# Expert weights carried in the scattered rows, and gathers that accumulate into x

## The chip, the cores and the metric

The kernel runs on one core of a Trainium2 chip. The metric is the device time of one execution in microseconds, the median of several runs. Engines are named as in the profile: PE is TensorE (PEld its weight loads), DVE is VectorE, ACT is ScalarE, POOL is GpSimd, SP is SyncE, which only issues transfers here.

## The reference

Two transformer blocks on 8 sequences of 512 tokens, 256 features each. Each block is pre-normalized attention (16 heads of 16) and a pre-normalized mixture of experts, both added to x.

```
x = x + L0_attention(layernorm(x))           # causal, rope, 4 key/value heads
x = x + L0_experts(layernorm(x))             # 32 experts of 96, top 8 of softmax
x = x + L1_attention(layernorm(x))           # causal, 16 heads, biases
x = x + L1_experts(layernorm(x))             # 16 experts of 176, top 2, and a shared expert of 352

# experts, both layers; layer 0 divides the 8 weights by their sum
rw, sel = top_k(softmax(x @ router.T), K)
for e in experts:
    w_e = sum(where(sel == e, rw, 0))
    acc = acc + (silu(x @ wg[e]) * (x @ wu[e])) @ wd[e] * w_e
```

## The kernel before

The kernel computes only the chosen experts. Each layer goes in two stages, so that the program has four of them, with the results at the end:

- **Attention 0** (0 to about 656 us of the profile). `pipeline` runs over the 8 sequences. While the heads of sequence b are computed (24 steps: scores on PE, exponentials on ACT, masks on DVE L658), `before(b + 1)` prepares the next sequence and `finish(b - 1)` ends the last: output projection, then `after0`, which normalizes (`layernorm`), turns the rows and calls `route`.
- **route** (L313) computes the router's logits, chooses the experts and gives every pair of token and expert a row in a buffer in device memory (`lay.xg`), where each expert has a slab of its own. POOL scatters the normalized rows there: for each block of 128 tokens and each of the k experts one indirect transfer of 128 rows of 256 numbers (L384), 32 for a sequence of layer 0 and 8 of layer 1. After that, DVE finds the weight of each of the k rows by comparing the rows' numbers with those of all experts (`same`, L394 to L399) and keeps them in `lay.weights`.
- **Experts 0** (`experts`, about 656 to 1172 us). A job is two tiles of 128 rows. Five stages follow one another with lags of 0, 4, 5, 6 and 7 steps: `load` (SP reads the tiles from `lay.xg`; every 8 tiles, expert numbers become register values that address the weights), `turn_x` (PE transposes, DVE copies), `gate_up` (PE; ACT takes silu, DVE multiplies with the other half, L1141 in layer 0 and L1138 in layer 1), `turn_h` (PE, DVE), `down` (PE, ACT copies, SP writes the rows to `lay.yg`). The order on PE is the order of the program here (a manual schedule); on the other engines a planner orders instructions by their dependencies and priorities. Sequences are in two parts (4 and 4 in layer 0, 5 and 3 in layer 1), so that the results of the first part can be collected while the second is computed. `Beside` spreads this work over the steps.
- **Collecting**. `gathers` (L1183) has POOL fetch the k result rows of each token with an indirect transfer of 128 rows (L1199) into a small ring of tiles, and `add` (L1205) has DVE multiply by the weights and add to x (L1210). `gathered` keeps `AHEAD` = 4 pairs of gathers waiting for their adds. `add` may be ordered behind a given DVE instruction (`behind`): the last copy of the experts, or the last mask of the attention. For layer 0, the first four sequences are collected during the experts (`x_in_ring`), the others during attention 1 (`ahead1`), two sequences ahead of where they are used. In layer 1, `results` also turns x and writes the output.
- **Attention 1** (about 1172 to 1770 us), as attention 0, with the shared expert in `after1`. At its start POOL fills the tiles of v with ones (`v_tiles`, L791), for which it needs memory that the experts release.
- **Experts 1 and the results** (from 1770 us to the end at 2055.8).

[...] The tiles of x are a ring of four; sequences that are not in it stand in device memory (`x_after`).

Of the kernel before, what the change touches and what calls it, by code (L numbers as in the profile page):

```python
# [7 lines left out]
F32 = mybir.dt.float32  # L8
# [64 lines left out]
AHEAD = 4  # L73
# [18 lines left out]
def two_blocks_kernel(  # L92
# [56 lines left out]
    zeros = cpool.tile([P, D], F32, tag="zeros", name="zeros")  # L149
# [60 lines left out]
    class Layer:  # L210
        def __init__(self, n, part, seqs, n_e, k, gu):
# [10 lines left out]
            self.xg = drp.tile([n_e * self.cap + P, D], F32, tag=f"xg{name}", name=f"xg{name}")  # L222
# [16 lines left out]
            self.weights = routes("weights", k, F32)  # L239
# [41 lines left out]
    def layernorm(x, lnp, name, tag="xn", bufs=1):  # L281

        stats = lnp.tile([P, NT, 6], F32, tag="stats", name=f"stats_{name}")
        mv = lnp.tile([P, NT, 2], F32, tag="mv", name=f"mv_{name}")
        for t in range(NT):
            nc.vector.bn_stats(out=stats[:, t, :], in_=x[:, t, :])
            nc.vector.bn_aggr(out=mv[:, t, :], in_=stats[:, t, :])
        rstd = inverse_root(mv[:, :, 1], lnp, name)
        xn = lnp.tile([P, NT, D], F32, tag=tag, name=f"xn_{name}", bufs=bufs)
        for t in range(NT):  # L290
            nc.vector.tensor_scalar(
                xn[:, t, :], x[:, t, :], mv[:, t, 0:1], rstd[:, t : t + 1], ALU.subtract, ALU.mult
            )
        return xn
# [17 lines left out]
    def ffn_parts(smp, bank):  # L312
        def route(n, b, xn, xT, name, again):  # L313
# [36 lines left out]
            wt = smp.tile([P, NT, n_e], F32, tag="wt", name=f"wt_{name}")  # L350
# [31 lines left out]
            for t in range(NT):  # L382
# [7 lines left out]
            yield  # L390

            same = smp.tile([P, NT, k, n_e], F32, tag="same", name=f"same_{name}", bufs=1)
            shape = [P, NT, k, n_e]
            nc.vector.tensor_tensor(  # L394
                same, key.unsqueeze(2).to_broadcast(shape), keys[:, :, :k].unsqueeze(3).to_broadcast(shape), ALU.is_equal
            )
            nc.vector.tensor_tensor(same, same, wt.unsqueeze(2).to_broadcast(shape), ALU.mult)
            weights = lay.weights[b]
            nc.vector.tensor_reduce(weights, same, AX.X, ALU.add)  # L399
# [224 lines left out]
    class Attention:  # L624
# [6 lines left out]
        def __init__(self, n, late, ptp, ps, bank, wo):  # L631
            self.n, self.fine, self.late, self.ptp, self.ps, self.bank, self.wo = n, fines[n], late, ptp, ps, bank, wo
            self.heads, self.otok, self.rec = {}, {}, {}
            self.last = iter(())
            self.masked = None
# [107 lines left out]
    def pipeline(att, before, after, n_before, n_after, till, ahead=None):  # L743
# [12 lines left out]
        for b in range(NB):  # L756
# [4 lines left out]
            for n, _ in enumerate(att.steps(b)):  # L761
                while made_post < n_after * (n + 1 - STEPS) // (till - STEPS):
                    next(post, None)
                    made_post += 1
                while made_pre < n_before * (n + 1) // (n_steps - 2):
                    next(pre, None)
                    made_pre += 1
                next(early, None)
# [162 lines left out]
    def fast1(w, v1s, lnp, atp, late, ptp, ps, bank):  # L931
        wv, wo, vb, ob, qkb = (w[n] for n in ("v", "o", "vb", "ob", "qkb"))
        att = Attention(1, late, ptp, ps, bank, wo)

        def before(b):
            x, name = xs[b], f"a1_{b}"
            xn = layernorm(x, lnp, name)
# [42 lines left out]
    def tables(lay, small, bank, again, beside=None):  # L980
# [3 lines left out]
        lay.offi = tpool.tile([1, 2, most], I32, tag=f"offi{lay.part}", name=f"offi{name}")[:, :, :n_t]  # L984
# [41 lines left out]
        offf = small.tile([1, 2, n_t], F32, tag="offf", name=f"offf_{name}", bufs=1)  # L1026
        dn = D if lay.n == 0 else ND1 * D
        nc.vector.tensor_scalar(offf[:, 0, :], ex, float(n_e - 1), float(lay.gu), ALU.min, ALU.mult)
        nc.vector.tensor_scalar(offf[:, 1, :], ex, float(n_e - 1), float(dn), ALU.min, ALU.mult)
# [3 lines left out]
        for lo in range(0, n_e, 8):  # L1033
            with tc.issue_after(beside.load) if beside else ExitStack():
# [5 lines left out]
                for rows in at:  # L1040
                    inst = nc.sync.dma_start(out=lay.xg[rows, :], in_=zeros)
                    tc.declare_no_dep(inst.ins, group=group, reason="these rows are no token's")
                    tc.add_to_no_dep_group(group, inst.ins)
            yield

    class Beside:


        def __init__(self, *items):
            self.items = []  # L1050
            for item in items:
                self.add(*item)
            self.last = None
            self.load = None
# [16 lines left out]
    def experts(n, gu, dn, mp, ps, again, beside):  # L1071
# [10 lines left out]
        def registers(lay, i):  # L1082
# [7 lines left out]
                    lay.offi[0:1, j, i : min(i + RB, lay.tiles(again))], engines=[ENG.PE], min_val=0, max_val=(lay.n_e - 1) * step,  # L1090
                    skip_runtime_bounds_check_because="an expert's number is at most the last one's",
                )[1]
                for j, step in enumerate((lay.gu, w_dn))
# [6 lines left out]
        def load(lay, i):  # L1100
# [3 lines left out]
            xg = mp.tile([P, 2, D], F32, tag="xg", name=f"xg_{name}_{part}_{i}", bufs=6)  # L1104
# [4 lines left out]
        def turn_x(lay, i):  # L1109
            part = lay.part  # L1110
            xg = made.pop(("xg", part, i))
# [8 lines left out]
        def gate_up(lay, i):  # L1120
            part = lay.part
            xT = made.pop(("xT", part, i))
# [4 lines left out]
            else:  # L1127
                gus = [ps.tile([P, 2 * inner], F32, tag="gu", name=f"gu_{name}_{part}_{i + j}") for j in range(2)]
            for j in range(2):
# [6 lines left out]
                if n:  # L1136
                    nc.scalar.activation(h[:, j, :], gus[j][:, :inner], AF.Silu)
                    nc.vector.tensor_tensor(h[:, j, :], h[:, j, :], gus[j][:, inner:], ALU.mult)  # L1138
            if n == 0:
                nc.scalar.activation(h, whole[:, :, :inner], AF.Silu)  # L1140
                nc.vector.tensor_tensor(h, h, whole[:, :, inner:], ALU.mult)  # L1141
# [39 lines left out]
    PART = 2  # L1181

    def gathers(n, b, gat, again=""):  # L1183
# [11 lines left out]
        for t in range(NT):  # L1195
            for lo in range(0, k, PART):
                g = gat.tile([P, PART, D], F32, tag="gath", name=f"g{name}_{t}_{lo}")
                for i in range(PART):
                    nc.gpsimd.indirect_dma_start(  # L1199
                        out=g[:, i, :], out_offset=None, in_=lay.yg[: lay.tiles(bool(again)) * P, :],  # L1200
                        in_offset=bass.IndirectOffsetOnAxis(ap=rows[:, t, lo + i : lo + i + 1], axis=0),
                    )
                yield b, t, lo, g, lay.weights[b]

    def add(part, behind):  # L1205

        b, t, lo, g, weights = part
        with tc.issue_after(behind()) if behind() else ExitStack():
            for i in range(PART):
                nc.vector.scalar_tensor_tensor(  # L1210
                    xs[b][:, t, :], g[:, i, :], weights[:, t, lo + i : lo + i + 1], xs[b][:, t, :], ALU.mult, ALU.add
                )

    def gathered(n, b, gat, again="", behind=lambda: None):

        wait = []
        made = gathers(n, b, gat, again)
        while True:
            if len(wait) == AHEAD:
                add(wait.pop(0), behind)  # L1220
            part = next(made, None)
            if part is None:
                break
            wait.append(part)
            yield
        while wait:
            add(wait.pop(0), behind)
            yield
# [50 lines left out]
    def results(seqs, gat, op, ps, again="", behind=lambda: None):  # L1279


        def begin(b):
            fetch_x(b, x_after[1], f"c1{again}")
            yield from gathers(1, b, gat, again)

        made = {}
        for b, after in zip(seqs, [*seqs[1:], None]):
            if b not in made:
                made[b] = []
                for part in begin(b):  # L1290
                    made[b].append(part)
                    yield
            if after is not None:
                made[after] = []
                for part in begin(after):
                    made[after].append(part)
                    yield
            for part in made.pop(b):
                add(part, behind)
                yield  # L1300
# [43 lines left out]
    def all_experts(n, gw, gat, again=False, weights=()):  # L1344
# [6 lines left out]
        with ExitStack() as s:  # L1351
# [11 lines left out]
            def behind():  # L1363
                return beside.last

            def x_in_ring():
                for b in range(SPLIT[0]):
                    fetch_x(b, x_after[0], f"a1{g}")
                    yield from gathered(0, b, gat, g, behind)
# [22 lines left out]
            if n == 0:  # L1392
                beside.add(done, end, SPLIT[0] * 21, x_in_ring())
            else:
                beside.add(done, end, SPLIT[1] * 10, results(range(SPLIT[1]), gat, gat, ps, g, behind))
            experts(n, gw, dw, mp, ps, again, beside)


    PARTS = 4
    with ExitStack() as s:  # L1400
# [6 lines left out]
        def after0(b):  # L1407
            name = f"f0_{b}"
            kept = keep_x(b, x_after[0]) if b < NB - 1 else None
            xn = layernorm(xs[b], lnp, name, "xn_rows", 2)  # L1410
# [14 lines left out]
    with ExitStack() as s1:  # L1425
        wp1 = s1.enter_context(tc.tile_pool(name="attn_w1", bufs=1, reuse_waits="tile"))
        gat = s1.enter_context(tc.tile_pool(name="gather", bufs=AHEAD, reuse_waits="tile"))
        w1, loads1 = weights1(wp1)
        all_experts(0, gw0, gat, weights=loads1)
        with ExitStack() as s:  # L1430
# [3 lines left out]
            att, before = fast1(w1, v1s, lnp, atp, late, ptp, ps, bank)  # L1434
# [3 lines left out]
            def ahead1(b):  # L1438
                if b >= SPLIT[0]:
# [3 lines left out]
                    yield from gathered(0, b, gat, behind=lambda: att.masked)  # L1443

            def after1(b):
                name = f"f1_{b}"
                xn = layernorm(xs[b], lnp, name, "xn_rows")
# [9 lines left out]
            pipeline(att, before, after1, 15, 17, NCK * STEPS, ahead1)  # L1457
# [3 lines left out]
    def last_part(gw, again=""):  # L1461
        with ExitStack() as s:
            gat = s.enter_context(tc.tile_pool(name=f"gather1{again}", bufs=2 * NT, reuse_waits="tile"))
# [8 lines left out]
    def general0():  # L1472
        with ExitStack() as s:
# [8 lines left out]
            def all_of(b, name):  # L1482
# [3 lines left out]
                xn = layernorm(xs[b], lnp, name)  # L1486
# [7 lines left out]
    def general1(gat):  # L1494
        with ExitStack() as s:
# [20 lines left out]
            def all_of(b, name):  # L1516
                if b >= SPLIT[0]:
                    fetch_x(b, x_after[0], "a1g")
                    yield from gathered(0, b, gat, "g")
                yield from attention1(b, w)  # L1520
                xn = layernorm(xs[b], lnp, name)
# [13 lines left out]
    with tc.If(v != 0):  # L1535
        with ExitStack() as s:
            gat = s.enter_context(tc.tile_pool(name="gatherg", bufs=AHEAD, reuse_waits="tile"))
# [166 lines left out]
```

## Time and profile before

| | us |
|---|---|
| median of 3 runs | 1711.17 |
| lowest, highest | 1704.48, 1711.67 |
| the profiled execution | 2057.66 |
| its span | 2055.8 |

The profiled execution is longer than the timed ones. Busy times by stage are these, in us (gathers and scatters are POOL's indirect transfers in that stretch):

| stretch | PE | DVE | ACT | POOL | transfers of POOL | DMA share |
|---|---|---|---|---|---|---|
| attention 0, 0 to 656 | 396.6 | 339.0 | 205.5 | 247.3 | 242 scatters | 0.28 |
| attention 1, 1150 to 1770 | 552.2 | 366.1 | 255.7 | 199.1 | 128 gathers, 64 scatters | 0.26 |
| experts 1, 1770 to 1930 | 154.3 | 68.7 | 35.8 | 13.5 | 15 gathers | 0.42 |
| the end, 1930 to 2056 | 83.7 | 53.2 | 25.7 | 48.6 | 50 gathers | 0.48 |

The columns are busy time; matmuls are pipelined, and the ends of their records are modelled. The DMA share is the mean busy share of the core's 16 DMA engines.

### The profile page before, as it was taken

How to read it: one execution, taken by the hardware profiler on the slowest of the kernel's cores; microseconds unless marked ns; L12 is line 12 of the kernel's file. 1: busy time of each engine (PE TensorE's matmuls, PEld its weight loads, DVE VectorE, ACT ScalarE, POOL GpSimd, SP SyncE). 2: the span in 40 equal slices, each digit the busy share in tenths (PEclk: the TensorE clock that was granted, in tenths of full speed). 3: DMA queues.
4: the chain of work that ended last, by engine and by line, in shares of the span. 5: the costliest groups of instructions: out<-in, count | busy, mean ns of one | idle time of the engine just before them, and what ended most of it. 6: DMA issues, size and time to landing. Idle time of an engine off the chain costs nothing.

```text
span 2055.8 us, 31001 instructions
## 1 busy us (share of the span) xinstructions
PE 1619.5 (79%) x10180; PEld 1070.6 (52%) x10180; DVE 1088.5 (53%) x3311; ACT 649.2 (32%) x867; POOL 645.7 (31%) x662
## 2 busy tenths in 40 slices
PE   5967467477533799997988989788897998999892
PEld 3424234233212699987877735444443545677671
DVE  5657256266342444445766546667566554543352
ACT  3524234234210233322222254343342454122121
POOL 0052452442565000015444301545444111100434
PEclk9978688687775899999999999898998998999995
DMA  1123233321224567667777500332332212443454
GB/s 60 40 93 85 85 95 106 127 73 57 93 97 151 159 224 229 188 186 209 219 213 215 171 8 22 111 113 72 111 101 63 79 42 70 151 144 114 136 172 136
DMA packets 230552, 247.73 MB, mean 121 GB/s; under 512 B 80212, under 2 KB 203220, under 8 KB 230388
## 3 DMA queue, kind: packets, MB, share of 16 engines
q1 hardware_dynamic: 199172, 160.88, 25.8%
q0 software_dynamic: 30720, 83.93, 12.8%
q8 instruction: 89, 1.46, 0.3%
q10 hardware_dynamic: 496, 0.85, 0.1%
q14 instruction: 75, 0.61, 0.1%
HBM read 127.06 MB, written 118.49 MB: 119 GB/s over the span
## 4 chain that ended last, share of the span: by engine, by line
PE 58%; another core or an unknown queue 8%; DVE 8%; issue 6%; ACT 2%; DMA 1%; ACTq 0%; SPq 0%; DVEq 0%
PE gu_m L1132 14%; PE y_m L1162 10%; PE st_a L647 5%; PE xgT_m L1115 4%; PE o_a L670 4%; PE hT_m L1151 3%; PE sg_f L411 2%; PE sy_f L424 2%; PE su_f L411 2%; PE q_a L963 2%; PE y_a L736 2%; PE lg_f L320 1%; PE k_a L968 1%; PE v_a L950 1%
## 5 line engine op out<-in xcount | busy, mean ns | idle before, releaser
L1199 POOL DMA_INDIRECT g<-yg,yrows x320 | 315.5, 986 | 705.0 <-DMA xg_m<-xg 231.2
L384 POOL DMA_INDIRECT xg<-xn_f,rows_f x320 | 325.3, 1017 | 671.5 <-DVE rows_f L381 336.6
L652 ACT ACTIVATE p_a<-st_a 128x2048 f32<-128x2048 f32 (+1 forms) x192 | 305.9, 1593 | 434.6 <-PE st_a L647 228.9
L1132 PE MATMUL gu_m<-gw,xgTs_m 128*128 x1552 | 348.6, 370 | 28.5 <-DVE xgTs_m L1117 14.5
L647 PE MATMUL st_a<-qT_a,kT_a 32*128 32x512 f32 (+3 forms) x2048 | 214.4, 504 | 122.4 <-ACT p_a L652 68.4
L1132 PEld LDWEIGHTS gu_m<-gw,xgTs_m 128*128 128x128 f32 x1552 | 268.4, 199 | 60.9 <-issue 19.9
L1162 PE MATMUL y_m<-dw,hTs_m 96*128 (+1 forms) x952 | 244.8, 388 | 1.5 <-DVE hTs_m L1152 1.5
L670 PE MATMUL o_a<-p_a,v 128*32 128x512 f32 (+3 forms) x2048 | 206.3, 479 | 18.6 <-DVE p_a L658 11.8
L658 DVE TENSOR_TENSOR p_a<-p_a,causal 128x512 f32<-128x512 f32 x256 | 170.3, 682 | 87.5 <-ACT p_a L652 70.3
L647 PEld LDWEIGHTS st_a<-qT_a,kT_a 32*128 32x128 f32 x2048 | 95.1, 200 | 228.4 <-issue 107.9
L1117 DVE COPY xgTs_m<-xgT_m 128x512 f32<-128x512 f32 x194 | 133.5, 688 | 147.7 <-PE xgT_m L1115 102.4
L1167 ACT COPY ys_m<-y_m 128x512 f32<-128x512 f32 x194 | 113.6, 585 | 239.9 <-PE y_m L1162 148.9
L1162 PEld LDWEIGHTS y_m<-dw,hTs_m 96*128 96x128 f32 (+1 forms) x952 | 170.0, 195 | 18.3 <-DVE hTs_m L1152 1.8
L1152 DVE COPY hTs_m<-hT_m 96x256 f32<-96x256 f32 (+1 forms) x194 | 92.7, 478 | 129.2 <-PE hT_m L1151 85.7
L1115 PE MATMUL xgT_m<-ident,xg_m 128*128 128x128 f32 x776 | 122.8, 281 | 17.6 <-DMA xg_m<-xg 12.6
L1140 ACT ACTIVATE h_m<-gu_m 128x192 f32<-128x192 f32 x150 | 49.5, 331 | 254.4 <-PE gu_m L1132 142.7
L1210 DVE SCALAR_TENSOR_TENSOR x_a<-g,weights,x_a 128x256 f32<-128x256 f32 x256 | 122.1, 477 | 4.1 <-issue 0.6
L670 PEld LDWEIGHTS o_a<-p_a,v 128*32 128x32 f32 x2048 | 52.2, 113 | 137.8 <-issue 88.7
L1115 PEld LDWEIGHTS xgT_m<-ident,xg_m 128*128 128x128 f32 x776 | 99.1, 145 | 42.3 <-issue 17.0
L1151 PE MATMUL hT_m<-ident,h_m 128*96 128x128 f32 (+1 forms) x476 | 87.4, 282 | 40.8 <-DVE h_m L1141 19.4
L676 DVE COPY osb_a<-o_a 128x512 f32<-128x512 f32 x64 | 43.9, 687 | 137.1 <-remote 93.2
L736 PE MATMUL y_a<-wo,oT_a 128*128 128x256 f32 x256 | 75.1, 431 | 39.4 <-ACT oT_a L729 37.7
(203 smaller groups left out, 1775.5 us busy)
## 6 DMA issues: line engine op xcount, KB each, us to landing
xg_m<-xg SPq DMA_DIRECT2D x388, 128.0 KB
yg<-ys_m SPq DMA_DIRECT2D x194, 256.0 KB
xg<-zeros SPq DMA_DIRECT2D x100, 128.0 KB
xg<-xn_f,rows_f POOLq DMA_INDIRECT x320
g<-yg,yrows POOLq DMA_INDIRECT x320
xf<-in_x_dram SPq DMA_DIRECT2D x8, 512.0 KB
x_after<-x_in SPq DMA_DIRECT2D x8, 512.0 KB
x_a<-x_after SPq DMA_DIRECT2D x8, 512.0 KB
```

The lines of the kernel that those rows point to most:

```text
L384: inst = nc.gpsimd.indirect_dma_start(out=lay.xg, out_offset=bass.IndirectOffsetOnAxis(ap=rows[:, t, i : i + 1], axis=0), in_=xn[:, t, :], ...
L647: nc.tensor.matmul(st[:, g, at : at + T - j * P], kT[r, j * P : (j + 1) * P], qT[r, j * P :], start=True, stop=True,)
L652: nc.scalar.activation(pt, st[:, :, :width], AF.Exp, scale=SCALE)
L658: self.masked = nc.vector.tensor_tensor(d, d, causal.unsqueeze(1).to_broadcast([P, NG, P]), ALU.mult).ins
L670: nc.tensor.matmul(o[32 * g : 32 * g + 32, j * P :], v1[:, j, v_at + g * (DH + 1) :][:, :32], probs[n][:, g, at : at + T - j * P], start=( ...
L1115: nc.tensor.transpose(tr[:, j, c, :], xg[:, j, c * P : (c + 1) * P], ident)
L1117: nc.vector.tensor_copy(xT, tr)
L1132: nc.tensor.matmul(gus[j], xT[:, j, c, :], gu[:, bass.ds(at + c * 2 * inner, 2 * inner)], start=(c == 0), stop=(c == ND - 1),)
L1151: nc.tensor.transpose(hp[:n_in, q, j, :], h[:, j, lo : lo + n_in], ident)
L1162: nc.tensor.matmul(y[:, j, :], hT[:n_in, q, j, :], dn[:n_in, bass.ds(at + q * D, D)], start=(q == 0), stop=(q == n_ch - 1),)
L1199: nc.gpsimd.indirect_dma_start(out=g[:, i, :], out_offset=None, in_=lay.yg[: lay.tiles(bool(again)) * P, :], in_offset=bass.IndirectOffset ...
L1210: nc.vector.scalar_tensor_tensor(xs[b][:, t, :], g[:, i, :], weights[:, t, lo + i : lo + i + 1], xs[b][:, t, :], ALU.mult, ALU.add)
```

## The change

- The buffer's rows become D + n_e wide (288 numbers in layer 0, 272 in layer 1). `layernorm` leaves n_e columns spare, `route` writes the token's weights of all experts there, and the scatter carries them along. The search for the k weights on DVE is gone, and so is `lay.weights`.
- In `gate_up` the product of silu and the other half is also multiplied by the weight of the row. The column is the tile's expert, a register value, which is now loaded on DVE too. In layer 0 one instruction for two tiles becomes two.
- The tiles that `load` reads are kept until `gate_up`; seven buffers instead of six.
- Layer 0's gathers accumulate straight into x in the DMA (`compute_op=ALU.add`), in the order expert rank, then block of 128 tokens. There is no ring of tiles and no add on DVE. In the experts' stage, all four sequences' x is fetched first.
- In layer 1's results, gathers stay plain, into whole tiles of four blocks for each of the two ranks, and DVE adds two blocks at a time without a weight.
- The first normalization of layer 1's attention is ordered behind masks: its statistics come after the last mask that was traced (for the first sequence, after the last copy of layer 0's experts). `before` starts four steps later in a sequence.

```diff
-            self.xg = drp.tile([n_e * self.cap + P, D], F32, tag=f"xg{name}", name=f"xg{name}")
+            self.width = D + n_e
+            self.xg = drp.tile([n_e * self.cap + P, self.width], F32, tag=f"xg{name}", name=f"xg{name}")
...
         for t in range(NT):
-            nc.vector.bn_stats(out=stats[:, t, :], in_=x[:, t, :])
+            with tc.issue_after(behind) if behind else ExitStack():
+                nc.vector.bn_stats(out=stats[:, t, :], in_=x[:, t, :])
...
-            wt = smp.tile([P, NT, n_e], F32, tag="wt", name=f"wt_{name}")
+            wt = xn[:, :, D : D + n_e]
...
-            same = smp.tile([P, NT, k, n_e], F32, tag="same", name=f"same_{name}", bufs=1)
...
-            nc.vector.tensor_reduce(weights, same, AX.X, ALU.add)
...
-                while made_pre < n_before * (n + 1) // (n_steps - 2):
+                while made_pre < n_before * (n + 1 - lead) // (n_steps - 2 - lead):
...
-            xg = mp.tile([P, 2, D], F32, tag="xg", name=f"xg_{name}_{part}_{i}", bufs=6)
+            xg = mp.tile([P, 2, lay.width], F32, tag="xg", name=f"xg_{name}_{part}_{i}", bufs=7)
...
+            def scaled(j):
+                nc.vector.scalar_tensor_tensor(
+                    h[:, j, :], h[:, j, :], xg[:, j, D:][:, bass.ds(offs[part, i + j][2], 1)], gus[j][:, inner:],
+                    ALU.mult, ALU.mult,
+                )
...
             if n == 0:
                 nc.scalar.activation(h, whole[:, :, :inner], AF.Silu)
-                nc.vector.tensor_tensor(h, h, whole[:, :, inner:], ALU.mult)
+                for j in range(2):
+                    scaled(j)
...
-        for t in range(NT):
-            for lo in range(0, k, PART):
-                g = gat.tile([P, PART, D], F32, tag="gath", name=f"g{name}_{t}_{lo}")
-                for i in range(PART):
-                    nc.gpsimd.indirect_dma_start(
...
+        for i in range(k):
+            for t in range(NT):
+                yield i, t, lay.yg[: lay.tiles(bool(again)) * P, :], bass.IndirectOffsetOnAxis(ap=rows[:, t, i : i + 1], axis=0)
+
+    def gathers(n, b, gat, again=""):
+        for i, t, yg, rows in gather_rows(n, b, gat, again):
+            nc.gpsimd.indirect_dma_start(
+                out=xs[b][:, t, :], out_offset=None, in_=yg, in_offset=rows, compute_op=ALU.add
+            )
+            if t % 2:
+                yield
...
-    def add(part, behind):
-        b, t, lo, g, weights = part
-        with tc.issue_after(behind()) if behind() else ExitStack():
-            for i in range(PART):
-                nc.vector.scalar_tensor_tensor(
-                    xs[b][:, t, :], g[:, i, :], weights[:, t, lo + i : lo + i + 1], xs[b][:, t, :], ALU.mult, ALU.add
-                )
...
+            made[b] = [gat.tile([P, NT, D], F32, tag="gath", name=f"g1{again}_{b}_{i}", bufs=2 * K1) for i in range(K1)]
...
+                    with tc.issue_after(behind()) if behind() else ExitStack():
+                        nc.vector.tensor_tensor(
+                            xs[b][:, lo : lo + 2, :], xs[b][:, lo : lo + 2, :], g[:, lo : lo + 2, :], ALU.add
+                        )
...
                 for b in range(SPLIT[0]):
                     fetch_x(b, x_after[0], f"a1{g}")
-                    yield from gathered(0, b, gat, g, behind)
+                yield
+                for b in range(SPLIT[0]):
+                    yield from gathers(0, b, gat, g)
...
-            pipeline(att, before, after1, 15, 17, NCK * STEPS, ahead1)
+            pipeline(att, before, after1, 15, 17, NCK * STEPS, ahead1, 4)
```

## The prediction

> **What bounds the kernel now.** I read the page first (busy shares, slices), then the chain that ended last, the busy time by stage, the groups of the operations that change, and the timeline where POOL hands over from one stage to the next.
>
> ```profile
> span 2055.8 us, 31001 instructions
> ...
> PE 1619.5 (79%) x10180; PEld 1070.6 (52%) x10180; DVE 1088.5 (53%) x3311; ACT 649.2 (32%) x867; POOL 645.7 (31%) x662
> ...
> PE   5967467477533799997988989788897998999892
> ...
> POOL 0052452442565000015444301545444111100434
> ```
>
> PE has most of the time, and its slices are low just where POOL's are not zero. By stage (us, then busy time of PE, PEld, DVE, ACT, POOL, the granted clock, the DMA share, GB/s):
>
> ```profile
> 690.00:905.00 215.00, 210.90 (x1330) 195.02 (x1329) 106.96 (x260) 66.59 (x147) 0.34 (x1) 0.99 0.66 202
> 905.00:1150.00 245.00, 207.20 (x1164) 184.82 (x1163) 148.28 (x377) 56.99 (x128) 123.53 (x128) 0.92 0.72 212
> ```
>
> ```profile
> 1441.30:1521.80 80.50, 68.61 (x417) 35.50 (x417) 51.34 (x162) 31.04 (x28) 40.76 (x41) 0.89 0.34 97
> ...
> 1602.70:1667.00 64.30, 64.08 (x431) 33.34 (x427) 35.24 (x120) 30.87 (x28) 8.99 (x9) 0.97 0.10 36
> ```
>
> The first pair is layer 0's experts without and with gathers, the second pair one sequence of layer 1's attention with and without. Without gathers PE is 98% and 99.7% busy. A step of the experts is then 2.825 us (distance of L1141 in the timeline); with gathers the mean is 245 us over 64 steps, 3.83. So gathers with their adds cost 64 x 1.0 = 61 us there and 4 x 16 = 65 us in attention.
>
> What does it, POOL's transfers or DVE's adds? The chain has long pieces in the scatter phases of attention 0, where there is no add at all:
>
> ```profile
> 374.30 21.23 another core or an unknown queue
> ...
> 530.21 23.46 another core or an unknown queue
> ```
>
> POOL issues 32 scatters without a pause from 349.6 to 391.3 and from 507.5 to 549.6; PE, ACT and DVE stand still until about 4 us after such a run. Runs of 8 to 12 gathers bring halts of 3 to 7 us. Most of the loss is therefore POOL's runs, the smaller part DVE. The profiled execution takes 2057.66 us, 346 more than the median of 1711.17. The halts of eight scatter runs (gaps in PE over 4 us before 690: 210 us) and the 126 us above make 336, so I take the timed executions to have little of them; they are then PE's at full step rate, with about 209 us (74 x 2.825) for the second half of layer 0's experts. I add differences in us to the median unscaled.
>
> **The operations concerned.**
>
> ```profile
> L1199 POOL DMA_INDIRECT g<-yg,yrows x320 | 315.5, 986 | 705.0 <-DMA xg_m<-xg 231.2
> ...
> L1210 DVE SCALAR_TENSOR_TENSOR x_a<-g,weights,x_a 128x256 f32<-128x256 f32 x256 | 122.1, 477 | 4.1 <-issue 0.6
> ```
>
> ```profile
> 2011.90 0.94 POOL L1199 DMA_INDIRECT g<-yg,yrows  x1 [24.08 <-DMA yg<-ys_m]
> ...
> 2014.61 0.48 DVE L1210 SCALAR_TENSOR_TENSOR x_c<-g,weights,x_c 128x256 f32<-128x256 f32 x1 [8.72 <-DMA g<-yg,yrows]
> ```
>
> A plain gather holds POOL 0.95 us and 0.30 follow; its data are usable 2.7 us after its start when nothing else moves. In the experts the shortest distance from a gather to its add is 3.9 us.
>
> **What the Trainium skill says.** "DMA: Bandwidth & Descriptors", Rules for kernel authors: an accumulating DMA reads its destination and writes it later, and what lands in between is lost, so one waits for the earlier DMA's semaphore. So the eight gathers of a row become a chain; no run here shows one yet. "Collectives: The Full Stack", The bandwidth ceiling: an add in the DMA engines takes two source reads, with two read descriptors per chunk, and half the rate; said of reduce-scatter, not seen here. "Perfetto Trace Analysis", DMA Instruction — SWDGE: POOL's record ends when the last descriptor is written, not when data land; the 1.8 us between the two lines above agree.
>
> **The change part by part.**
> 1. Adds of layer 0 go: 256 x 0.477 = 122 us of DVE. In attention 1 that is 32 x 0.477 = 15 us for each of four sequences, whose excess is 16 us, 6 to 7 of which is one common halt; of the other 9 I take 5 each: -20 (bounds -36 and 0). In the experts' second half PE's gaps ended by DVE sum to 22 us, half of them in common halts: -10 (-22 and 0).
> 2. The weights by equality go (L394, L397, L399): 24 x 1.22 = 29 us of DVE in layer 0, 3.65 per sequence, behind the scatters' rows, so nothing waits for them but later masks: 1 us each, -8 (-29 and 0). Layer 1's 6.7 us: 0.
> 3. The expert's product takes the weight. Between 128x192 (341 ns) and 128x512 (682 ns) an element costs 1.07 ns; 96 of them with the STT's surplus are about 306 ns, twice for 341: 150 x 0.27 = 41 us more DVE in layer 0. A step then has 0.69 + 0.42 + 0.61 = 1.72 us of DVE below PE's 2.825: 0, hidden by PE. The 388 offsets now also loaded on DVE: PE loads twice as many with its step constant (0); "Runtime: NRT & Kernel Launch", Instruction fetch mechanics, prices a register load from HBM at 0.2 us, here 1.6 us in four steps against 4.4 idle: still 0; if that cover went, up to 78 us.
> 4. Rows of 288 and 272 numbers for 256: loads of 144 KB for 128, 4.9 MB in layer 0, 24 us of DMA at 202 GB/s inside 450 us at a share of 0.66: 0, since seven buffers for six keep the lead although a tile is held one step longer. Scatters have the same rows and descriptors: 0, up to +10 in the halts.
> 5. Four fetches of x (512 KB each) queue on SP at once, 2 MB or 10 us at 202 GB/s, before experts' loads that run four steps (11 us) ahead: +2 (0 and +10).
> 6. The first normalization of layer 1 moves behind the last copy of the experts. Before, its statistics ran at 1011 us, under the experts:
>
> ```profile
> 1169.30 0.42 DVE L1152 COPY hTs_m<-hT_m 96x256 f32<-96x256 f32 x1 [0.58 <-PE hT_m L1151]
> 1171.91 1.38 DVE L291 TENSOR_SCALAR xn_a<-x_a,mv_a,rstd_a 128x256 f32<-128x256 f32 x4 [2.19 <-PE xT_a L307]
> ```
>
> Afterwards 4 x (0.41 + 0.17) + 12 x 0.15 + 4 x 0.42 = 5.8 us lie between that copy and PE's next work: +5. The others lie behind masks in the midst of a sequence, starting four steps later: 0.
> 7. Gathers of layer 0 accumulate. Nothing on DVE paces them now (L1199 waited 149 us for L1210); a gather waits for that of its row four earlier. A group of four costs the longer of 4 x (I + 0.3) and I's landing chain; 32 groups precede the memset of v, which stands behind them on POOL and which attention 1 needs:
>
> ```profile
> 1148.46 0.94 POOL L1199 DMA_INDIRECT g<-yg,yrows  x1 [0.30 <-issue]
> 1167.85 1.05 POOL L791 MEMSET v<- 128x1148 f32 x1 [18.44 <-PE gu_m L1132]
> ```
>
> Before, POOL was done 19 us early. I is between 0.95 (as now) and 1.9 us (twice the read descriptors); I take 1.7: 8.0 us a group, 256 us, against about 215 in a timed run: +41 (0 at 0.95; +67 at 1.9). In attention 1 a sequence takes 8 x 8.0 + 8 scatters x 1.26 = 74 us against some 70; a lead of one sequence hides most: +8 (0 and +16). POOL without pauses under loaded DMA: +10 in halts (-10, because at most four are in flight, and +25).
> 8. Results of layer 1 stay plain gathers, 128x512 adds (about 0.68) for pairs of 0.48: in the tail the same 24 gathers x 1.25: 0.
>
> Sum: -20 - 10 - 8 + 2 + 5 + 41 + 8 + 10 = +28, on the profile 2056 + 28, on the median **1739 us**.
>
> **Rivals.**
> - *POOL keeps pace* (other side: faster). If I stays near 0.95 and landing under 5.6 us, a group is 5 to 6.7 us, 32 groups under 215, the memset is in time, and part 7 is 0: -38 + 7 = -31, 1680. For it: POOL's record is the same for scatter and gather, and 3.9 us is already a bound for loaded landing; against it: the second read. It decides at I = 1.4 us.
> - *Both cancel*: I about 1.35 with +10 of halts and some lateness, 1711 within 8.
> - *The chain is long*: a row's next gather starts only 11 us later, or the order is kept for a whole sequence and not for its rows. 32 x 11 = 352, +137 at the experts' end; attention 1 gets 98 us for 70, 4 x 28 less one sequence's lead, +42; with -31: 1859. For it: an untried kind of DMA beside a DMA share of 0.72; against it: the order in which the four row blocks alternate.
>
> **How the numbers follow.** Chances: slower as forecast 0.45, POOL keeps pace 0.36, both cancel 0.10, long chain 0.09. A measurement tells 0.5%, 8.5 us, from no change. So faster 0.36, same 0.10, slower 0.54. The range takes in the faster case with its bounds and the forecast up to I = 1.9 with the other upper ends, and leaves out the long chain: 1670 to 1795. The forecast's own range is 1722 to 1790.
>
> **What would show it.** L1199's mean near 1.7 us and POOL's memset after the last expert step (part 7); the step of experts still 2.825 us in the first half (3, 4); sequences with gathers nearer 64 than 80 us in attention 1 (1); a gap of 5 us on PE after the last copy (6). It is wrong if the accumulating gather holds POOL 1 us and the memset is free when the experts end.

## The result, and the profile after

The changed kernel takes 1731.85 us (median of 4 runs, 1725.55 to 1738.09), the kernel before 1709.89 (median of 4) in runs beside it: ratio 1.0134, 95% interval 1.009 to 1.0178. It is slower by 22 us; 1739 was forecast.

One thing has to be known before two numbers are compared: the kernel before takes 1709 us on chip 13 (median of 27 runs, 1698 to 1715) but 2074 and 2078 on chips 7 and 10 (16 runs, 2068 to 2082), where PE, ACT and DVE halt together, and its profiled execution (2057.66 us) belongs with the second group, while its timed runs and all that was measured for this result belong with the first.

The page of the changed kernel, busy shares and two rows of slices:

```profile
span 1729.5 us, 30935 instructions
...
PE 1548.1 (90%) x10180; PEld 1032.7 (60%) x10180; DVE 990.9 (57%) x3129; ACT 650.0 (38%) x865; POOL 792.1 (46%) x662
...
PE   5899999985999999999948999979899988999991
...
POOL 0027676677700005888870038888883111000625
```

POOL's two long blocks of 8 are the accumulating gathers of the experts and of attention 1. PE is at 9 under the first of them and falls only at its end. Stretches by stage (us, then busy time of PE, PEld, DVE, ACT, POOL, the granted clock, the DMA share, GB/s): layer 0's experts without gathers, with them, and two sequences of attention 1 with gathers:

```profile
450.00:660.00 210.00, 204.29 (x1265) 188.49 (x1266) 113.79 (x299) 63.82 (x140) 19.18 (x20) 0.98 0.76 228
662.00:880.00 218.00, 211.72 (x1310) 192.77 (x1309) 116.92 (x314) 67.83 (x147) 182.16 (x118) 0.98 1.08 260
1085.40:1157.80 72.40, 69.04 (x484) 35.66 (x484) 43.04 (x135) 35.22 (x33) 60.20 (x41) 0.98 0.64 123
1157.80:1229.90 72.10, 63.22 (x417) 32.71 (x416) 39.81 (x127) 31.14 (x29) 59.90 (x41) 0.93 0.59 110
```

PE is 97% busy in the experts with and without gathers and a step of them takes 2.83 us (median) in both, although the DMA share goes from 0.76 to 1.08 (it adds up the times of packets, and so can pass 1): the added traffic costs PE nothing there. The gathers' group, and what the added weight costs on DVE:

```profile
L1200 POOL DMA_INDIRECT x_a<-yg,yrows x256 | 403.6, 1577 | 282.1 <-DMA xg_m<-xg 186.6
...
L1123 DVE SCALAR_TENSOR_TENSOR h_m<-h_m,xg_m,gu_m 128x96 f32<-128x96 f32 (+1 forms) x388 | 114.8, 326 | 110.0 <-ACT h_m L1136 65.2
```

An accumulating gather holds POOL 1.58 us on average where a plain one took 0.99 in the kernel before. The end of the 128 gathers of the first four sequences, on POOL's timeline, and the same moments on PE's:

```profile
895.37 1.54 POOL L1200 DMA_INDIRECT x_a<-yg,yrows  x1 [0.31 <-issue]
897.21 1.54 POOL L1200 DMA_INDIRECT x_a<-yg,yrows  x1 [0.30 <-issue]
898.18 2.64 POOL L782 MEMSET v<- 128x1148 f32 x2
```

```profile
867.70 1.93 PE L1162 MATMUL y_m<-dw,hTs_m 96*128 x8
872.97 1.97 PE L308 MATMUL xT_a<-ident,xn_a 128*128 128x128 f32 x8 [3.35 <-DVE xn_a L292]
...
880.24 1.88 PE L954 MATMUL q_a<-xT_a,wq 128*128 128x512 f32 x4
900.76 2.90 PE L959 MATMUL k_a<-xT_a,wk 128*128 128x512 f32 x3 [18.65 <-DVE v L945]
```

The 128 gathers start 1.85 us apart from 661.8 us on (1.54 and 0.30), 237 us in all, and the fill of v stands behind the last of them. PE waits 18.6 us for it, by way of DVE, which then writes v into the filled tile (L945). The 3.35 us ahead of that are the normalization that now follows the experts' last copy. Two gaps of 8.3 and 7.8 us are in attention 1. (A second profile of the same kernel, taken for experiment 1, has 16.5 us ahead of L959 and three gaps in attention 1, of 7.9, 9.8 and 5.0 us.) The first of them on DVE and on PE:

```profile
1154.24 1.29 DVE L649 TENSOR_TENSOR p_a<-p_a,causal 128x512 f32<-128x512 f32 x2 [0.29 <-ACT p_a L643]
1159.68 0.43 DVE L287 BATCH_NORM_STATS2 stats_a<-x_a 128x6 f32<-128x256 f32 x1 [4.14 <-DMA x_a<-yg,yrows]
1160.83 0.43 DVE L287 BATCH_NORM_STATS2 stats_a<-x_a 128x6 f32<-128x256 f32 x1 [0.72 <-DMA x_a<-yg,yrows]
...
1164.65 0.43 DVE L287 BATCH_NORM_STATS2 stats_a<-x_a 128x6 f32<-128x256 f32 x1 [1.45 <-DMA x_a<-yg,yrows]
...
1165.40 0.69 DVE L649 TENSOR_TENSOR p_a<-p_a,causal 128x512 f32<-128x512 f32 x1
```

```profile
1157.40 0.44 PE L719 MATMUL oT_a<-ident,otok_a 128*128 128x128 f32 x2
1166.15 1.08 PE L661 MATMUL o_a<-p_a,v 128*32 128x256 f32 x8 [8.31 <-DVE p_a L649]
```

The next sequence's x gets its last gathers while its statistics already stand in DVE's queue. ACT has the mask's input ready at 1159.4 us, but the mask (L649) starts at 1165.4, behind four statistics that wait for POOL's deliveries; the last two come 1.9 us apart. PE waits for the mask. At the end, 46.5 us pass from the start of the last expert matmuls (1683.0) to the end of the program.

### The profile page after: what moved, and what is told of

The parts are those of the page before. It is cut to its first block, busy times and chain, and to the rows that moved or that the text cites. A ratio compares the mean times of both kernels' runs of the same rounds, so it can differ in the third digit from the quotient of the medians.

```text
span 1729.5 us, 30935 instructions
## 1 busy us (share of the span) xinstructions
PE 1548.1 (90%) x10180; PEld 1032.7 (60%) x10180; DVE 990.9 (57%) x3129; ACT 650.0 (38%) x865; POOL 792.1 (46%) x662
## 4 chain that ended last, share of the span: by engine, by line
PE 51%; POOL 23%; DVE 9%; issue 8%; DMA 5%; ACT 2%; SPq 2%; DVEq 0%; ACTq 0%; POOLq 0%
POOL x_a L1200 18%; PE gu_m L1131 12%; PE y_m L1162 8%; PE st_a L638 5%; PE o_a L661 5%; POOL xg L385 4%; PE xgT_m L1106 3%; PE hT_m L1151 2%; PE qkv_a L843 2%; PE sg_f L402 2%; DVE p_a L649 2%; DMA xg<-xn_f,rows_f 2%; PE sy_f L415 2%; ACT p_a L643 2%; PE su_f L402 1%
## 5 line engine op out<-in xcount | busy, mean ns | idle before, releaser
L1200 POOL DMA_INDIRECT x_a<-yg,yrows x256 | 403.6, 1577 | 282.1 <-DMA xg_m<-xg 186.6
L385 POOL DMA_INDIRECT xg<-xn_f,rows_f x320 | 321.7, 1005 | 438.2 <-DVE rows_f L382 221.1
L1131 PE MATMUL gu_m<-gw,xgTs_m 128*128 x1552 | 335.5, 360 | 4.9 <-DVE xgTs_m L1108 3.0
L1131 PEld LDWEIGHTS gu_m<-gw,xgTs_m 128*128 128x128 f32 x1552 | 258.7, 193 | 33.6 <-DVE xgTs_m L1108 3.2
L1162 PE MATMUL y_m<-dw,hTs_m 96*128 (+1 forms) x952 | 238.5, 380 | 0.0
L661 PE MATMUL o_a<-p_a,v 128*32 128x512 f32 (+3 forms) x2048 | 197.7, 456 | 26.0 <-DVE p_a L649 25.9
L638 PE MATMUL st_a<-qT_a,kT_a 32*128 32x512 f32 (+3 forms) x2048 | 206.3, 484 | 11.7 <-ACT p_a L643 11.5
L649 DVE TENSOR_TENSOR p_a<-p_a,causal 128x512 f32<-128x512 f32 x256 | 170.4, 684 | 56.5 <-ACT p_a L643 55.4
L1108 DVE COPY xgTs_m<-xgT_m 128x512 f32<-128x512 f32 x194 | 133.7, 689 | 108.5 <-PE xgT_m L1106 108.0
L1123 DVE SCALAR_TENSOR_TENSOR h_m<-h_m,xg_m,gu_m 128x96 f32<-128x96 f32 (+1 forms) x388 | 114.8, 326 | 110.0 <-ACT h_m L1136 65.2
L1162 PEld LDWEIGHTS y_m<-dw,hTs_m 96*128 96x128 f32 (+1 forms) x952 | 165.9, 190 | 15.3
L1262 POOL DMA_INDIRECT g<-yg,yrows x64 | 61.8, 966 | 205.2 <-DVE h_m L1123 148.6
L661 PEld LDWEIGHTS o_a<-p_a,v 128*32 128x32 f32 x2048 | 49.5, 110 | 128.4 <-issue 67.5
L1106 PEld LDWEIGHTS xgT_m<-ident,xg_m 128*128 128x128 f32 x776 | 95.9, 142 | 42.1 <-issue 18.7
```

The costliest lines, as they stand in the source:

```text
L385: inst = nc.gpsimd.indirect_dma_start(out=lay.xg, out_offset=bass.IndirectOffsetOnAxis(ap=rows[:, t, i : i + 1], axis=0), in_=xn[:, t, :], ...
L638: nc.tensor.matmul(st[:, g, at : at + T - j * P], kT[r, j * P : (j + 1) * P], qT[r, j * P :], start=True, stop=True,)
L649: self.masked = nc.vector.tensor_tensor(d, d, causal.unsqueeze(1).to_broadcast([P, NG, P]), ALU.mult).ins
L661: nc.tensor.matmul(o[32 * g : 32 * g + 32, j * P :], v1[:, j, v_at + g * (DH + 1) :][:, :32], probs[n][:, g, at : at + T - j * P], start=( ...
L1106: nc.tensor.transpose(tr[:, j, c, :], xg[:, j, c * P : (c + 1) * P], ident)
L1108: nc.vector.tensor_copy(xT, tr)
```

## The experiments

Two questions: is POOL's time for the accumulation what costs, and through which waits; and what are the halts that the forecast put a part of its sum on? "A chip that halts" is one of those on which the kernel before takes some 2074 us, and each ratio is to the kernel before on the same chip, beside it.

### 1. The fill of v on DVE, on two kinds of chip

```diff
-            nc.gpsimd.memset(v1, 1.0)
+            (nc.vector if heads == H else nc.gpsimd).memset(v1, 1.0)
```

First on a chip that halts, together with the kernel before once more:

> The changed kernel with the two fills of v (layer 1) on DVE instead of POOL. POOL theory: PE's gap of 18.6 us at the start of attention 1 is the fill waiting in POOL's queue behind the 128 accumulating gathers; without it 17 to 20 us go, 1712 to 1715 us, and the two gaps of 8 us on PE in the middle of attention 1 stay. Rival (DMA theory: the transfers of the gathers, not POOL's queue, hold the start of attention 1): less than 5 us go, 1727 us or more.

> The kernel before, unchanged, for a second profile. If the common halts of the first profile (PE, ACT and DVE standing still after a long run of POOL's transfers, about 336 us in all) belong to that one execution, this profile has a span near 1710 us and a step of the experts near 2.83 us with gathers too. If they belong to the kernel, the span is near 2050 us again.

Measured: 2023.86 us, before 2074.49, ratio 0.9758 (0.9728 to 0.9788). The run of before gave 2074.84, with the halts of its first profile. So halts were not a property of the one profiled execution, which the forecast had taken them to be; all timed executions there take as long as the profiled one. Then beside the changed kernel on the chip that does not halt:

> The changed kernel itself, beside the kernel before on the same chip, as the measure for the other three. Theory (the halts of all engines belong to some chips and to POOL's unpaused transfers): where before takes about 1710 us this takes about 1732, ratio 1.013; where before takes about 2074 with halts, this takes some 2040 (the kernel with v's fill on DVE took 2024 there, plus the 19 us that the fill costs), ratio 0.984, that is the change's sign differs from chip to chip. Rival (the change costs the same everywhere): ratio 1.013 on every chip.

> The changed kernel with the fill of v's ones on DVE instead of POOL, so that attention 1's start does not stand behind the 128 accumulating gathers. Theory (the 18.6 us gap of PE at the start of attention 1 is the whole cost there): 15 to 19 us less than the changed kernel, about 1714 where that takes 1732, and the gap of PE is gone. Rival (the accumulating gathers are POOL's bound in attention 1 too, and the gain is given back there): under 6 us less, and PE's gaps in attention 1 grow.

Measured: the changed kernel 1733.03 (ratio 1.0132, 1.0102 to 1.0163), with the fill on DVE 1713.95 (ratio 1.0035, 1.0019 to 1.005). One line of code is worth 19.1 us, and PE's timeline no longer has the gap (fill on DVE, chip 13):

```profile
879.16 1.88 PE L954 MATMUL q_a<-xT_a,wq 128*128 128x512 f32 x4
880.87 1.88 PE L959 MATMUL k_a<-xT_a,wk 128*128 128x512 f32 x4
882.59 1.88 PE L954 MATMUL q_a<-xT_a,wq 128*128 128x512 f32 x4
```

The rival, that attention 1 gives the gain back, falls. Gaps of 8.7, 8.2 and 4.0 us are still there. The changed kernel itself did not run on a chip that halts, so that its sign there is not measured. If the fill cost 19 us there too, it would take some 2043 us against 2074 (an estimate).

### 2. The sum left out, or made on DVE

```diff
-                out=xs[b][:, t, :], out_offset=None, in_=yg, in_offset=rows, compute_op=ALU.add
+                out=xs[b][:, t, :], out_offset=None, in_=yg, in_offset=rows
```

```diff
+        def add(lo, g):
+            with tc.issue_after(behind()) if behind() else ExitStack():
+                nc.vector.tensor_tensor(xs[b][:, lo : lo + 2, :], xs[b][:, lo : lo + 2, :], g, ALU.add)
...
+                g = gat.tile([P, 2, D], F32, tag="gath0", name=f"g0{again}_{b}_{i}_{t}", bufs=4)
+            nc.gpsimd.indirect_dma_start(out=g[:, t % 2, :], out_offset=None, in_=yg, in_offset=rows)
```

Both ran twice, and both times on a chip that halts:

> The changed kernel with plain gathers in place of the accumulating ones, into the same rows of x, in the same order and with the same waits: the sum over experts of layer 0 and the old x are left out of the result. POOL theory: POOL holds 0.95 us for each gather instead of 1.54, a gather takes 1.25 instead of 1.85, 128 take 160 us and end before the experts do; in attention 1 a sequence needs 50 us of POOL instead of 72; the start's gap (18.6 us) and the gaps of 8 us go: 1732 - 19 - 16 - some, 1688 to 1698 us. Rival (wider rows, the second instruction for the product, offsets on DVE or the later normalization make the loss): within 8 us of 1732.

> The changed kernel with layer 0's gathers plain into a ring of four pairs and added on DVE, 128x512 at a time without a weight (16 adds of about 0.68 us for a sequence). POOL theory: all the rest of the change is free or helps, so this is as fast as before or faster, 1695 to 1710 us. Rival (the rest of the change costs time): 1718 us or more.

> The changed kernel with plain gathers into the same rows of x; the sum of the eight results is left out, so that the output is not the reference's. Theory (what the change loses is the time that POOL is held by an accumulating gather, 1.54 us for 0.97): where before takes 1710, POOL is done with 128 gathers after 160 us, before v's fill is due, and both the 18.6 us gap and the two 8 us gaps go: 1732 - 35 = 1697. Rival 1 (POOL's unpaused transfers halt all engines on every chip when they come 1.25 us apart): 1800 or more. Rival 2 (the added traffic, not POOL's time, is the loss): as above, 1697, but with POOL's gathers still near 1.5 us. On a chip where before takes 2074: 2288, as once measured.

> Only the accumulation undone: plain gathers into a ring of four pairs and adds on DVE, behind the experts' last copy and the last mask; weights still in the scattered rows, normalizations still ordered. Theory (adds on DVE cost little where the engines do not halt, so that the other parts of the change gain what the accumulation loses): where before takes 1710, 1700 to 1706. Rival (the adds cost as the forecast took it, some 5 us a sequence in attention 1 and 10 in the experts): 1727. On a chip where before takes 2074: 2119, as once measured.

Measured, on chip 7 and on chip 10: without the sum 2288.18 and 2287.9 (ratios 1.1025, 1.0964 to 1.1085, and 1.1008, 1.0965 to 1.105); with plain gathers and adds 2119.31 and 2120.9 (1.0214, 1.015 to 1.0279, and 1.0201, 1.017 to 1.0233). The group and a stretch of PE's timeline without the sum (second run, chip 10):

```profile
L1200 POOL DMA_INDIRECT x_a<-yg,yrows x256 | 248.8, 972 | 386.0 <-DMA xg_m<-xg 229.7 <-issue 76.5 <-DVE p_a L649 39.5
```

```profile
983.28 2.93 PE L1131 MATMUL gu_m<-gw,xgTs_m 128*128 x8 [18.54 <-DVE xgTs_m L1108]
1010.53 0.67 PE L1151 MATMUL hT_m<-ident,h_m 128*96 128x128 f32 x2 [24.33 <-DVE h_m L1123]
```

Into the same rows of the same tiles, a gather without the sum holds POOL 0.97 us, so the sum itself adds 0.60 us. It also adds packets; the queue of POOL's transfers (packets, MB, share) in the changed kernel and without the sum:

```profile
q0 software_dynamic: 55296, 88.65, 22.7%
```

```profile
q0 software_dynamic: 30720, 88.65, 12.1%
```

Without the sum, the 128 gathers of the experts come 1.25 us apart without a pause, and PE loses 149 us in gaps of over 3 us between 938 and 1120 (150 in the first run, on chip 7). With the sum and the fill on DVE, on the same two chips (experiments 1 and 3), the same 128 transfers come 1.85 us apart, and PE has no gap over 4 us from 720 to 1140 us. The stretch from 940 to 1120 us on chip 10, without the sum and then with it (columns as above):

```profile
940.00:1120.00 180.00, 30.92 (x110) 24.47 (x109) 9.38 (x25) 5.30 (x12) 120.47 (x127) 0.53 0.38 110
```

```profile
940.00:1120.00 180.00, 178.68 (x1124) 163.40 (x1124) 96.80 (x249) 57.03 (x125) 150.40 (x98) 1.00 1.10 266
```

The DMA share is 0.38 where the engines halt and 1.10 where they do not, so full DMA engines are not what halts them. On these two chips the halts go with how closely POOL's transfers follow each other: at 1.85 us there are none in this stage, at 1.25 there are. Closeness alone is not enough, since on chip 13 the scatters of attention 0 come 1.26 us apart too (median), and PE has no gap over 3 us from 20 to 395 us. The distance alone was not changed either: packets differ as well. What halts the engines, no record names; the chain of waits calls it "another core or an unknown queue".

By halts one could also explain the 50 us by which the kernel with the fill on DVE is faster on chip 7 than the kernel before, whose gathers come 1.25 us apart between its pauses for the ring. That is not shown: of the 43.8 us for which PE stands idle in the kernel before from 910 to 1160 us there, only 18.7 are in gaps over 3 us, and DVE's adds are gone as well. With plain gathers and adds on DVE, that is with all of the change but the accumulation, the kernel is 43 to 45 us slower than before on these chips, where as fast or faster was first expected. By the traces of chip 10, experts 0 begin 20 us later than before and attention 1 takes some 36 us longer, while the experts with gathers are no slower; the cause is open. The price of the plain kernels on a chip without halts was expected, 1697 and 1700 to 1706, and is not measured.

On chip 10, beside them:

> The kernel before once more, for its trace. Theory (the halts belong to the chip): if the other kernels of this call show 1710 for before, no gap of over 4 us in attention 0, a step of 2.825 us for the experts with gathers too, and v's fill on POOL done before attention 1 needs it; otherwise halts as in the first profile.

It gave 2072.96 us with halts. A trace of before without halts is missing from this study.

### 3. The order of the first normalization, and an earlier start of the gathers

```diff
-            att, before = fast1(w1, v1s, lnp, atp, late, ptp, ps, bank, last)
+            att, before = fast1(w1, v1s, lnp, atp, late, ptp, ps, bank, None)
```

```diff
-        xs[b] = xpool.tile([P, NT, D], F32, tag="x", name=f"x_{name}_{b}", bufs=4)
+        xs[b] = xpool.tile([P, NT, D], F32, tag="x", name=f"x_{name}_{b}", bufs=5)
...
-            early = ahead(b + 2) if ahead and b + 2 < NB else iter(())
+            early = ahead(b + 3) if ahead and b + 3 < NB else iter(())
```

The first alone, then both, each with the fill on DVE, on the chip that does not halt:

> As the kernel with v's fill on DVE, and the first normalization of layer 1's attention no longer ordered behind the experts' last copy. Theory (the normalization alone lies between that copy and PE's next matmul, 3.3 us in the trace of after): 3 to 4 us less than the kernel with v's fill on DVE. Rival (what the order spares, a statistics instruction on DVE that waits for gathers in front of the experts' copies, costs more): 5 to 40 us more, with gaps of PE among the last steps of the experts.

> As the last, and x in a ring of five tiles with the gathers of sequences 4 to 7 begun one sequence earlier, so that POOL's idle 125 us at the start of attention 1 are used. Theory (the two 8 us gaps of PE in attention 1 come from gathers that finish too late for the statistics of the next sequence, which then hold up the masks): 14 to 18 us less than the last kernel, about 1695 where before takes 1710, and no gap over 4 us in attention 1. Rival (POOL's gathers are late because POOL is full, and an earlier start only moves them): within 4 us of the last kernel. Other rival (gathers earlier collide with the scatters of the sequences before): 5 to 15 us more.

Measured: 1773.62 (ratio 1.0371, 1.034 to 1.0403) and 1763.33 (1.0304, 1.0272 to 1.0336). The theory of the first fell: freeing the normalization costs 59.7 us where a gain of 3 was expected. DVE and PE of that kernel show why:

```profile
666.34 0.53 DVE L1123 SCALAR_TENSOR_TENSOR h_m<-h_m,xg_m,gu_m 128x96 f32<-128x96 f32 x2
726.11 0.43 DVE L287 BATCH_NORM_STATS2 stats_a<-x_a 128x6 f32<-128x256 f32 x1 [59.24 <-DMA x_a<-yg,yrows]
```

```profile
734.36 2.92 PE L1131 MATMUL gu_m<-gw,xgTs_m 128*128 x8 [64.27 <-DVE xgTs_m L1108]
```

Unordered, the planner places the statistics of sequence 0 amid the experts as soon as the gathers are issued, and DVE stands still until they land (32 x 1.85 = 59 for a sequence). A copy that PE needs (L1108) stands behind them in DVE's queue, and PE loses 64 us from 670 on. The order that the change brings along is therefore no cost of 3.3 us, but those 3.3 us in place of 64.

The ring of five with its earlier gathers gives 10.3 us against the first, less than the 14 to 18 expected, but past the 4 of the rival: no mask waits at L661 any more, two gaps of 5.0 and 6.2 us ahead of the experts' normalization (xT_f) have come. With the order kept, this is the version from which most was hoped:

> v's fill on DVE, x in a ring of five tiles, the gathers of sequences 4 to 7 one sequence earlier, and the order of the normalizations kept as in the changed kernel. Theory (the two 8 us gaps in attention 1 are late gathers; the ring took 10 us from the kernel without the order): on a chip where before takes 1710, 1704, ratio 0.996, no gap over 6 us in attention 1, and none of 64 us in the experts. Rival (the ring only helped because that kernel's gathers were late by other causes): 1710 to 1716.

It ran on a chip that halts: 2017.25 us against 2078.32, ratio 0.9717 (0.9689 to 0.9744), the lowest of the ratios on such chips, if hardly apart from 0.9758 of the fill alone. Its trace has no gap of PE over 4 us from 714 to 1352 us, and none of 64. Later in attention 1 three gaps of 8.1, 8.0 and 6.5 us follow, ended by ACT; for a chip without halts none over 6 was expected. On such a chip it was not tried. 1713.95 less 10.3 makes an estimate of 1704 us, which no run shows; there, no version has been shown to be faster than the kernel before.

## Why the prediction was right, point by point

- **Part 7, the gathers that precede the fill: right in mechanism, too large.** Forecast +41, measured 18.6 and 16.5 on two traces and 19.1 by removing it. The mis-sized term is I, 1.54 us for the 1.7 taken: the 128 gathers take 237 us for 256, which makes 19 of the 22 us between forecast and measurement. PE needed the fill 220 us after the first gather (at 882.1 us), where 215 were taken. The forecast's point of decision, I = 1.4, lies below what was measured, and so "POOL keeps pace" did not come true; at 0.97, by these numbers, 128 x 1.25 = 160 us would have been in time (an estimate).
- **The landing chain hardly ever bound.** A group of four takes 7.4 us, and the gathers keep 1.85 us throughout; the longest distance between two of the 128 is 2.3 us. The Trainium skill's rule in "DMA: Bandwidth & Descriptors", Rules for kernel authors, that an accumulating DMA waits for the earlier one to its destination, shows in this trace as five waits of POOL for an earlier gather, 1.6 us in all, among 256 gathers: with four row blocks in turn, each has the 7.4 us to land.
- **Where the extra time comes from.** The Trainium skill's "Collectives: The Full Stack", The bandwidth ceiling, gives two read descriptors for an add, in a reduce-scatter. What the profile counts here is packets: 96 more for each of 256 gathers, 144 in place of 48. It is the sum that adds them and not the wider rows, since the kernel without the sum has 30720 again. POOL's time rises by 0.60 us along with that, to 1.6 times; the forecast's upper end, twice, was not reached.
- **Attention 1: +8 forecast for a sequence of 74 us.** A sequence with gathers took 72 us, and POOL was at its limit as forecast. But the loss, 16.1 us in two gaps (22.6 in three on the second trace), comes from statistics that hold up masks on DVE. Part 6 put the normalizations behind masks in mid-sequence at zero; that step was wrong. The sign named for part 1, a sequence nearer 64 than 80 us, came out in the middle.
- **Part 6: +5 forecast, 3.3 measured.** It missed that without the order the kernel would lose 60 us.
- **Parts 1 and 2, the gains of 38.** By subtraction: 22 us measured, less 18.6, 16.1 and 3.3 leave -16 for all else (-19 with the second trace and its runs). How it divides is open, since no trace of before without halts exists. The 10 us in the experts were read from a trace with halts; in the changed kernel without halts PE is 97% busy both with gathers and without, and a kernel before that was equally full would have had nothing to gain there. A slip in the reading of the profile, 64 x 1.0 = 61 us where it is 64, changes no term of the sum.
- **Parts 3, 4 and 5: zero, or nearly.** The product with the weight takes 304 ns (median of the 300 of 128x96), 306 were worked out, and the experts' PE is full. The register loads on DVE were priced at 0.2 us each, by a figure for loads from HBM; the kernel loads from tiles on the chip, and on the trace one load of up to eight values takes 0.84 us (median of 50), about half the 1.6 worked out. The wider scattered rows may cost where engines halt: experts 0 begin at 667 to 678 us in six profiles of the four changed versions there against 645 to 656 in three of the kernel before; the forecast had up to 10 for it. Which edit does it wasn't tried.
- **Halts: +10 forecast, none in the measured runs.** That the timed executions have little of them held, and the 10 us that were added for them all the same did not come. The reason given did not hold: halts did not belong to one execution, as both later profiles of before have them.
- **Part 8: zero.** From the start of the last expert matmuls to the end the changed kernel takes 46.5 us, the kernel before 49.9 (2021.2 to 2071.1, third trace, on a chip that halts).

That the sum came so near (28 forecast, 22 measured) is in part luck, since both sides were too large: costs of 66 were forecast and 38 measured, gains of 38 forecast and 16 left by subtraction. The mechanism that decided, the fill behind POOL's longer gathers, was foreseen and is shown by experiment 1; the loss in attention 1 came by another way than forecast.

## What to carry to other kernels

Moving an add into the DMA took it from DVE and put 0.60 us more for each transfer on POOL, which issues them: multiply the longer hold by the number of transfers, and look for what is queued behind the last of them, here a fill that DVE could do as well. A consumer of data that many transfers build up is best placed by hand behind the work that shares its engine; left to the planner, it held that engine here for 59 us, until the data had landed. Before time is read off a trace with standstills of all engines, the traced run's own time has to be set beside the timed runs.

## What the hardware showed that was not expected

- The same program took 1709.49 us on chip 13 and 2074.49 and 2078.32 on chips 7 and 10, 365 to 369 us more, with common halts of PE, ACT and DVE under close runs of POOL's transfers. Each chip was used at one time only, so whether it is the chip or something else at that time is open. In attention 0 alone, experts begin at 425 us in the changed kernel where nothing halts and at 667 with the fill on DVE where engines do.
- On those chips a transfer that holds POOL longer (1.85 us from one to the next for 1.25) goes with a faster program: on chip 7, 2288 us without the sum, 2024 with it and the fill on DVE.
- A DMA share of 1.08 in a stage in which PE stays 97% busy.
